# A four-layer image network on one core: the gate products of layer 3 leave layer 1's turns for the stages around layer 0

## The chip, the core and the metric

The kernel is one launch on 1 core of one Trainium2 chip. The metric is device time in microseconds of a whole launch; a time given for a kernel is the median of several runs. Engines are named as in the profile: PE (TensorE, products), PEld (its weight loads), DVE (VectorE), ACT (ScalarE), POOL (GpSimd) and SP (SyncE, which here issues most DMAs).

## What is computed

The input is x of shape (4, 64, 64, 128) in float32: four images of 64 x 64 pixels with 128 channels. Four layers follow each other on each image.

- Layer 0: attention of each pixel to its 7 x 7 neighbours (4 heads of 32), times a sigmoid gate, plus the input.
- Layer 1: group norm, then full self-attention over the 4096 pixels, plus the input.
- Layer 2: a gated product with sums over image rows, an output product, and a layer norm.
- Layer 3: a block with a depthwise 3 x 3 convolution and a selective scan in four directions. The change concerns its second half of columns, z, and where it is made:

```python
def _L3_conv_ref(x, Win, conv_w, conv_b, Wxproj, ...):      # D_INNER = 256
    xz = x @ Win                                   # (4, 64, 64, 512)
    xb, z = jnp.split(xz, 2, axis=-1)
    xb = conv3x3_depthwise(xb, conv_w)             # 256 channels
    xb = jax.nn.silu(xb + conv_b)                  # "u" in the kernel
    ...                                            # x_dbl, four scans over the pixels: y
    y = (y0 + y1 + y2 + y3)
    zf = jax.nn.silu(z.reshape(Bb, L, Cd))         # the gate
    yz = y * zf
    ...                                            # layer norm over the 256 channels
    out = yn @ Wout
```

The gate z of a pixel needs only the output of layer 2 at that pixel, and it is not used before the scans are done.

## The kernel before

**Tiles.** An image is 4096 pixels by 128 channels, in 8 chunks of CH = 512 pixels, or NT = 32 tiles of 128. Layer 0 takes 32 blocks of 8 x 16 pixels in a pipelined loop, `for i in range(-3, NT + 5)`, in which scores, softmax, value products and the projection of neighbouring blocks overlap; it is a Python generator, of which the first 8 steps (`take_in` of two chunks) can be drawn ahead of the rest. Its last iterations make the statistics and the input hT of layer 1. Layer 1 starts with one chain: mean and variance of groups (`pm` L582, `pvar` L590), Sqrt (`sd` L593), `ga` L595, then normalised hT (L605) and the products for q, k and v (L607 to L614). Then 16 query blocks follow, each of 16 groups of score products (`sc` L638), a softmax whose exponentials stand in `st` (L665), and value products (`po` L674). The scores of one block and the values of the block before overlap.

**Turns.** Layer 1 calls `between(i)` after each 8 groups, with i from 0 to 33; the main loop calls it for the turns after layer 1 (34 to 37, between pairs of `take_in` steps of the next image; for the last image 34 to 42). A turn holds other layers' work that lies beside layer 1's products: one of the four parts of layer 2 for one chunk (`turn`, `mix`, `add`, `norm`: transposes, gates, an output product, Sqrt, then the chunk x3 stored to memory, L783), and one part of layer 3's front. Layer 2 starts at turn 6, so chunk n of image b is complete from turn 4n + 9 on, and the last ones after layer 1.

**Layer 3's front.** `front(b)` returns `turn(i)`. In image b's layer 1 it works at chunks 4 to 7 of image b-1 and 0 to 3 of image b, four turns for each: `load` fetches x3 of the chunk from memory into xc (L816), `project` makes the first half of the products (`pi` L822) and copies them to xh, `convolve` runs the convolution: nine taps of a chunk on ACT (`begin` L865, `multiply` L880 and L884), on POOL (L892) and on DVE (`add_taps` L901). In the chunk's fourth turn, `gate` makes the two products `pz` (L851), applies Silu (`zf` L843) and stores zf (L855), and the next chunk's xc is loaded. Seven turns after its start, `activate` makes u by Silu (L843), `lower` the product for x_dbl (`pd` L963, `dq` L968, stores at L970), a broadcast row `bb` loaded back or made by PE, du (L983, stored into y by SP, or added into it by POOL), and `times_b` makes u times B and stores it (L994). Layer 3's second half runs after all images and reads these from memory.

The last image's chunks 4 to 7 are handled by `end(i)`, which makes their gates from x3k, still on the chip; the change leaves these four as they are. `takes` says which chunks' projections belong to which four turns; image b's front takes (b-1,4) and (b-1,5) in turn 0. `front(b)` and `turn(-1)`, which loads xc for these two, come after layer 0 of image b is issued.

**Order.** The program is a list of instructions for each engine, made from the order of the Python calls by a scheduler which may move instructions of one engine past each other; those marked `keep_in_program_order` keep their order among each other. Layer 0's instructions carry this mark (`pin`), and so do the Silu activations of `gate` and `activate` (L842 to L845), so that u and zf keep the order of the source. An engine works through its list in order; one waiting instruction holds those behind it. An activation function from another table than the one before costs an ACT_TABLE_LOAD; Silu, Sqrt and Exp each bring their own here.

**Buffers.** The pool `tmp` hands out buffers by tag in turn. Tag "c512" has 9 buffers of 128 x 512 float32 (256 KB) for prT (layer 0), x2T, sg, o and x3 (layer 2), and gsum, zf, du, u1 and bb (layer 3). A tile that gets a buffer waits for what last read it, be it an engine or a store. The products share three rings in PSUM; `pz`, `pi`, `pq`, `pk`, `pg`, `pl`, `py` and `sc` use the one with 4 buffers.

Of the kernel before, what the change touches and what calls it, by code (L numbers as in the profile page):

```python
# [22 lines left out]
F32 = mybir.dt.float32  # L23
# [6 lines left out]
P = 128  # L30
B, H, W, C = 4, 64, 64, 128
L = H * W
NT = L // P
BR, BC = 8, 16
CH = 512
# [103 lines left out]
def layers_0_to_2(  # L139
    ctx, tc, xf, mata, matb, rows, rpb, convw, sel, ident, cl, dram, big, ring, early, x3_d, ub_d, zf_d, y_d, dbl_d, ct_d, gw_d, bw_d  # L140
):
    nc = tc.nc
    wp = ctx.enter_context(tc.tile_pool(name="wa", bufs=1))
    tmp = ctx.enter_context(tc.tile_pool(name="tmp", bufs=2))
# [216 lines left out]
    def layer_0(b, xt, edge_t):  # L361
# [7 lines left out]
        gate = sml.tile([P, NT], F32, name="gate", tag="gate", bufs=2)  # L369
# [4 lines left out]
        def pin(ins):  # L374
            return tc.keep_in_program_order(ins)
# [61 lines left out]
        def statistics(n):  # L437
            pin(nc.vector.bn_stats(st[:, n, :], hT[:, bass.ts(n, CH)]))
# [106 lines left out]
        for i in range(-3, NT + 5):  # L545
            if i + 3 < NT:
                score(i + 3)
            if b == 0 and i < 1:
                load_x(0, xt, (4 * i + 28, 4 * i + 32), kept=True)
            if 0 <= i - 1 < NT:  # L550
                value(i - 1)
            if 0 <= i + 1 < NT:
                normalise(i + 1)
            if 0 <= i - 2 < NT:
                project(i - 2)
            if 0 <= i < NT:
                by_key(i, 0, nc.scalar.copy)
                by_key(i, 1, nc.vector.tensor_copy)
            if 0 <= i + 2 < NT:
                soften(i + 2, (0, 1))  # L560
            n, part = divmod(i + 3, 4)
            if n + 2 < NCH or (n + 2, part) == (NCH, 0):
                take_in(n + 2, part)
            if 0 <= i < NT:
                by_key(i, 2, nc.scalar.copy)
            if 0 <= i + 2 < NT:
                soften(i + 2, (2, 3))

            n, part = divmod(i - 6, 4)
            if 0 <= n < NCH and part == 0:  # L570
                hand_on(n)
            if 0 <= n < NCH and part == (1 if n < NCH - 1 else 0):
                statistics(n)
        handed[b] = hT, st


# [216 lines left out]
    def by_image_rows(t):  # L793
        return t.rearrange("p (i j) -> p i j", j=W)

    def front(b):
# [1 line left out]
        xh = wp.tile([P, 2, 2, RC + 2, W], F32, name="xh", tag="be")  # L798
        accs = [wp.tile([P, 2, CH], F32, name=f"acc{k}", tag=f"bm{2 * k}") for k in range(2)]
        u0 = wp.tile([P, 2, CH], F32, name="u0", tag="bm1")  # L800
        x_of, parts_of, sums, u_of = {}, [], {}, {}

        def at_end(i, n):
            return i == B - 1 and n >= 4
# [6 lines left out]
        def load(i, n):  # L811
            if at_end(i, n):
                x_of[i, n] = fresh.pop(n)
                return
            x = x_of[i, n] = tmp.tile([P, CH], F32, name="xc", tag="g1")
            nc.sync.dma_start(x, x3_d[i][:, bass.ts(n, CH)])  # L816

        def project(i, n):
            me = n & 1
            for f in range(2):  # L820
                pi = ps_s([P, CH], "pi")
                nc.tensor.matmul(pi, lhsT=win[:, P * f:P * f + P], rhs=x_of[i, n], start=True, stop=True)  # L822
                nc.scalar.copy(xh[:, me, f, 1:RC + 1, :], by_image_rows(pi))
            row = nc.vector if at_end(i, n) and n > 5 else nc.gpsimd
            if n == 4 and i < b:
                nc.gpsimd.tensor_copy(xh[:, me, :, 0, :], kept_row)
            elif n > 0:
                row.tensor_copy(xh[:, me, :, 0, :], xh[:, 1 - me, :, RC, :])
                row.tensor_copy(xh[:, 1 - me, :, RC + 1, :], xh[:, me, :, 1, :])
# [15 lines left out]
                tc.keep_in_program_order(ins)  # L845

        def gate(i, n):
            x = x_of.pop((i, n))
            for f in range(2):
                pz = ps_s([P, CH], "pz")  # L850
                nc.tensor.matmul(pz, lhsT=win[:, DI + P * f:DI + P * f + P], rhs=x, start=True, stop=True)  # L851
                zf = tmp.tile([P, CH], F32, name="zf", tag="c512", bufs=9)

                silu(i, n, zf, pz)
                nc.sync.dma_start(zf_d[i][f][:, bass.ts(n, CH)], zf)  # L855

        def tap(n, f, dy, dx):
            r0, r1, c0, c1 = region(n, dy, dx)
# [137 lines left out]
        def turn_c(i, part):  # L996

            if part == 0:
                ct = x_of["c"] = tmp.tile([W, 2, W], F32, name="ct", tag="gb")
                nc.sync.dma_start(ct[:, 0, :], by_image_rows(dbl_d[i][RANK + 1:RANK + 2, :])[0])  # L1000
            else:
                ct = x_of.pop("c")
                pt = ps_t([W, W], "pt3")
                nc.tensor.transpose(pt, ct[:, 0, :], ident[0:W, 0:W])
                nc.scalar.copy(ct[:, 1, :], pt)
                nc.sync.dma_start(by_image_rows(ct_d[i])[0], ct[:, 1, :])
# [25 lines left out]
        takes = [[(b - 1, 4), (b - 1, 5)], [(b - 1, 6)], [(b - 1, 7)]] if b > 0 else [[], [], []]  # L1032
# [12 lines left out]
        def end(i):  # L1045
# [6 lines left out]
            if i == 31:  # L1052
                gate(c, 5)
# [39 lines left out]
        def turn(i):  # L1093

            j, r = divmod(i, 4)
            add_parts()
            if i == -1:
                for c in takes[0]:
                    load(*c)
                return  # L1100
            now = whole[j] if j < 8 else None
            if j < 8:
                if r == 0:
                    for c in takes[j]:
                        project(*c)
                    if j == 7 and b < B - 1:
                        project_row(b, 4)
                if now and j < 7:
                    convolve(*now, (r // 2,), r & 1)
                elif now and r < 2:  # L1110
                    convolve(*now, range(2), r)
                if r == 3:
                    for c in takes[j]:
                        gate(*c)
                    for c in takes[j + 1] if j < 7 else []:
                        load(*c)

            for k, at in ((0, 16), (2, 28), (4, 32)):
                if i == at and whole[k] and whole[k][0] & 1:
                    copy_du(*whole[k])  # L1120
            if b > 0 and i == 8 and (b - 1) & 1:
                copy_du(b - 1, 2)

            for c, at in zip(whole, u_at):
                if c and i == at:
                    activate(*c, at >= 32)
                if c and i == at + 1:
                    lower(*c)
                if c and i == at + 2 and not by_product(*c):
                    times_b(*c, x_of.pop((*c, "b")), nc.gpsimd)  # L1130
            if b > 0 and i in (22, 24):
                turn_c(b - 1, (i - 22) // 2)
            if b == 0 and i == 3:
                output_weights()
            if b == B - 1 and i == 6:
                diagonals()
            if b == B - 1:
                end(i)

        return turn  # L1140

    coming = layer_0(0, x_next, edge_of[0])
    for _ in range(8):
# [2 lines left out]
    ahead = [x_next]  # L1146
    for b in range(B):
        xt = ahead.pop(0)
        for _ in coming:
            pass  # L1150
        if b == 0:
            for t, d in zip(bias_m, bias_d):
                nc.sync.dma_start(d, t)
        parts = layer_2(b, xt)

        def between(i):

            n, part = divmod(i - 6, 4)
            if i == 6 and b + 1 < B:
                ahead.append(load_x(b + 1))  # L1160
            if i >= 6 and n < NCH:
                parts[part](n)
            first_part(i)
            if b + 1 < B and i == NT + 1:
                edge_of[b + 1] = edge_bias(0)
            if b + 1 < B and i == NT + 3:
                bias_m[:] = bias_tiles()
                for t, d in zip(bias_m, bias_d):
                    nc.sync.dma_start(t, d)

        first_part = front(b)
        first_part(-1)
        layer_1(b, xt, *handed.pop(b), between)
        if b + 1 < B:
            coming = layer_0(b + 1, ahead[0], edge_of[b + 1])
        for i in range(NT + 2, NT + 6 if b + 1 < B else NT + 11):
            between(i)
            if b + 1 < B:
                next(coming)
                next(coming)  # L1180
# [380 lines left out]
```

## Time and profile before

| | before |
|---|---|
| median of 3 runs | 3655.63 us (3653.8 to 3657.22) |
| the profiled execution | 3657.49 us, of which the span of instructions is 3655.7 us |
| granted PE clock, mean | 0.915 |
| PE, ACT, DVE busy | 3293.8, 2619.3, 2773.2 us |
| layer 1 of images 0 to 3, first score to last value product | 525.3, 541.4, 540.9, 546.3 us |
| from there to the next image's first layer 0 score | 22.2, 24.0, 23.1 us |
| after image 3's layer 1, to the first product of the scan stage | 62.8 us (2957.2 to 3020.0) |
| last softmax of layer 0 to layer 1's first score, images 1 to 3 | 36.2, 35.0, 34.9 us |

The page gives for each engine its busy time and its share of the span, then the span in 40 equal slices of 91.4 us with the busy share in tenths. The four blocks of layer 1 fill most of the first 33 slices, and the scans the last seven. Durations used below are those of single instructions in this one execution. In the lists by line and in the timelines, an arrow with an engine and a line after an idle time names what released the waiting instruction. A product of 512 columns stands as two records of about 0.59 us that overlap.

### The profile page before, as it was taken

Reading aid. Unit: us, or ns where it says so; the run is one execution under the profiler, and the core shown is the slowest. Engines: PE = TensorE matmul, PEld = TensorE weight load, DVE = VectorE, ACT = ScalarE, POOL = GpSimd, SP = SyncE. Lnnn points to the kernel's source line nnn. Section 1 sums busy time; section 2 is a strip of 40 time slices with the busy share of each in tenths; the row PEclk is TensorE's granted clock in tenths of the full one; section 3 lists DMA queues with packets and bytes.
Section 4 is the critical chain, followed back from the end, with each engine's and each line's share of the span. In section 5 each row is a group of like instructions: output and inputs, shape, how many; then the busy total and the mean of one; then the engine's idle time right before and its main releaser. Section 6 shows DMA issues by size and latency. Waiting matters only on the chain. (4 is left out here: it accounts for less than half of the span.)

```text
span 3655.7 us, 61448 instructions
## 1 busy us (share of the span) xinstructions
PE 3293.8 (90%) x22234; PEld 2603.0 (71%) x22234; DVE 2773.2 (76%) x5070; ACT 2619.3 (72%) x4324; POOL 1416.7 (39%) x1592
## 2 busy tenths in 40 slices
PE   7999999999999999998999999989999987666647
PEld 4679988866788888666888886668888852222246
DVE  5757777767768777677787776767877768999968
ACT  4855667778667777686676777866767759999934
POOL 6500012245112222451122224521222338999856
PEclk8999999999999999999999999999999995555579
DMA  4200000131001012410021213100100279999998
GB/s 123 73 25 3 12 18 27 54 100 35 24 27 45 27 45 87 135 39 24 24 79 30 77 54 101 40 1 24 45 30 34 69 225 211 214 238 217 201 275 284
DMA packets 189362, 310.38 MB, mean 85 GB/s; under 512 B 23007, under 2 KB 111996, under 8 KB 184156
## 3 DMA queue, kind: packets, MB, share of 16 engines
q1 hardware_dynamic: 146260, 220.27, 18.0%
q0 software_dynamic: 24384, 76.95, 11.9%
q10 hardware_dynamic: 18416, 9.24, 0.9%
q8 instruction: 176, 2.88, 0.3%
q14 instruction: 126, 1.03, 0.1%
HBM read 167.69 MB, written 155.56 MB: 88 GB/s over the span
## 5 line engine op out<-in xcount | busy, mean ns | idle before, releaser
L674 PEld LDWEIGHTS po<-v,st 128*128 128x128 f32 x8192 | 1049.2, 193 | 73.5 <-issue 35.7
L674 PE MATMUL po<-v,st 128*128 128x129 f32 x8192 | 1067.8, 277 | 17.6 <-ACT st L665 17.6
L638 PE MATMUL sc<-qT,kT 128*128 128x256 f32 x4096 | 1025.7, 382 | 12.7 <-DVE mx L644 12.5
L642 ACT COPY st<-sc 128x512 f32<-128x512 f32 x1024 | 580.5, 587 | 454.2 <-PE sc L638 452.6
L644 DVE TENSOR_TENSOR mx<-mx,sc 128x512 f32<-128x512 f32 x896 | 613.2, 684 | 275.7 <-ACT st L642 252.3
L638 PEld LDWEIGHTS sc<-qT,kT 128*128 128x128 f32 x4096 | 718.9, 191 | 105.7 <-issue 13.9
L664 DVE TENSOR_TENSOR st<-st,pb 128x2048 f32<-128x2048 f32 x256 | 572.4, 2280 | 29.0 <-PE pb L661 28.7
L665 ACT ACTIVATE st<-st 128x2048 f32<-128x2048 f32 x256 | 484.6, 1910 | 28.5 <-DVE st L664 27.2
L1271 PE MATMUL pdt<-dbl,dt 8*128 8x512 f32 x512 | 307.5, 1081 | 142.3 <-ACT de L1278 141.7
L1282 POOL TENSOR_TENSOR inp<-de,ub 128x1024 f32<-128x1024 f32 x128 | 409.6, 4391 | 6.8 <-ACT de L1278 6.3
L1271 PEld LDWEIGHTS pdt<-dbl,dt 8*128 8x128 f32 x512 | 114.2, 312 | 332.8 <-ACT de L1278 270.0
L505 POOL TENSOR_SCALAR pr<-pr,sm 128x308 f32<-128x308 f32 (+3 forms) x512 | 243.9, 496 | 205.1 <-DVE sm L503 186.8
L746 POOL TENSOR_TENSOR x<-x,row 128x512 f32<-128x512 f32 x32 | 47.9, 1498 | 707.1 <-DVE mx L644 686.7
L892 POOL TENSOR_TENSOR gsum<-gsum,tp 128x504 f32<-128x504 f32 (+1 forms) x177 | 229.2, 1301 | 127.1 <-ACT gsum L880 73.8
L497 ACT ACTIVATE pr<-pr,mx 128x308 f32<-128x308 f32 (+3 forms) x512 | 262.8, 517 | 1.3 <-DVE mx L486 1.3
L1309 DVE TENSOR_TENSOR_SCAN h<-h,end,inp 128x1024 f32<-128x1024 f32 x96 | 221.1, 2346 | 20.3 <-ACT h L1295 9.7
L514 PE MATMUL pt<-ident,pr 128*88 128x128 f32 (+5 forms) x1472 | 205.4, 276 | 9.8 <-ACT prT L516 8.8
L901 DVE SCALAR_TENSOR_TENSOR acc<-xh,cc,acc 128x512 f32<-128x512 f32 (+3 forms) x250 | 199.5, 803 | 10.2 <-ACT acc L865 8.6
L1324 POOL DMA_DIRECT2D y<-yo x112 | 200.6, 2710 | 13.1 <-DMA y<-y 4.8
L742 POOL TENSOR_TENSOR o<-o,rt 128x512 f32<-128x512 f32 x32 | 34.3, 1070 | 438.9 <-DVE o L741 434.4
L514 PEld LDWEIGHTS pt<-ident,pr 128*88 128x88 f32 (+5 forms) x1472 | 164.6, 138 | 45.2 <-ACT prT L516 25.9
L483 DVE CUSTOM_DVE_ANT_0 pr<-sc,bias_m 128x266 f32<-128x266 f32 (+1 forms) x384 | 152.1, 452 | 56.7 <-PE sc L479 55.1
(235 smaller groups left out, 4964.8 us busy)
## 6 DMA issues: line engine op xcount, KB each, us to landing
y<-yo POOLq DMA_DIRECT2D x112, 512.0 KB, 10.4
y<-y SPq DMA_DIRECT2D x48, 512.0 KB
zf_d<-zf SPq DMA_DIRECT2D x64, 256.0 KB
ub_d<-u SPq DMA_DIRECT2D x64, 256.0 KB
ub<-ub_d SPq DMA_DIRECT2D x16, 1024.0 KB
yl<-y SPq DMA_DIRECT2D x64, 256.0 KB
zc<-zf_d SPq DMA_DIRECT2D x64, 256.0 KB
v_d<-vg SPq DMA_DIRECT2D x128, 64.0 KB
```

Source lines behind the costliest of these rows:

```text
L497: pin(nc.scalar.activation(k.pr[:, h], k.pr[:, h], AF.Exp, bias=k.mx[:, h:h + 1], accum_out=k.sm[:, h:h + 1]))
L505: nc.gpsimd.tensor_scalar(k.pr[:, h], k.pr[:, h], k.sm[:, h:h + 1], 1.0, ALU.mult, ALU.mult)
L514: pin(nc.tensor.transpose(pt[0:n, h, :], k.pr[:, h, at:at + n], ident))
L638: nc.tensor.matmul(ps[:, r, :], lhsT=kT[:, bass.ts(G * g + r, P)], rhs=qT[:, bass.ts(i, QB)], start=True, stop=True)
L642: nc.scalar.copy(st, ps)
L644: nc.vector.tensor_tensor(k.mx, group(ng * i) if g == 1 else k.mx, ps, ALU.max)
L664: nc.vector.tensor_tensor(part, part, pb.unsqueeze(1).to_broadcast([P, 4 * G, QB]), ALU.add)
L665: nc.scalar.activation(part, part, AF.Exp)
L674: nc.tensor.matmul(k.po[:, h, :], lhsT=st[:, r, bass.ts(h, P)], rhs=v[:, j, :], start=(j == 0 and h == 0), stop=(j == NT - 1 and h == 1))
L892: nc.gpsimd.tensor_tensor(a, a, p, ALU.add)
L1271: nc.tensor.matmul(pdt[j][:, g, :], lhsT=dt[o:o + RANK, P * f:P * f + P], rhs=at(dbl[o:o + RANK, :], k & 2, g0, g0 + CH), start=True, stop ...
L1282: nc.gpsimd.tensor_tensor(by_rows(inp), by_rows(de), at(ub_s[f], b ^ (k & 1), SC * n, SC * n + SC), ALU.mult)
```

## The change

- 28 of the 32 chunks' gates move: all but those of the last image's chunks 4 to 7.
- Gates of (b, 0 to 3) go to turns 34 to 37 (NT + 2 to NT + 5), that is after image b's layer 1. Gates of (b-1, 4 to 7) go to iterations NT - 1 to NT + 2 of image b's layer 0, near its end.
- Since xc is given up after its projection, a new function `fetch` loads x3 of the chunk once more into a tile xg, tag "c512": 28 more DMAs of 256 KB on SP, at turns 32 and 33 (two each) and at iterations NT - 3 (two), NT - 1 and NT (one each).
- The projection of (b-1, 4) goes from turn 0 to iteration NT + 2 of layer 0. `front(b)` for b > 0 is made at iteration NT - 4, and xc for its first two chunks is loaded at NT - 3.
- To make this possible, `layer_0` yields i at the end of each iteration below NT + 4.

```diff
@@ layer_0
                 statistics(n)
+            if i < NT + 4:
+                yield i
@@ front: project
+            if not at_end(i, n):
+                x_of.pop((i, n))
@@ front: gate
-            x = x_of.pop((i, n))
+            x = x_of.pop((i, n)) if at_end(i, n) else fetched.pop((i, n))
@@ front: new
+        def fetch(i, n):
+            x = fetched[i, n] = tmp.tile([P, CH], F32, name="xg", tag="c512", bufs=9)
+            nc.sync.dma_start(x, x3_d[i][:, bass.ts(n, CH)])
@@ front: turn
-            if i == -1:
-                for c in takes[0]:
-                    load(*c)
-                return
...
                     for c in takes[j]:
-                        project(*c)
+                        if c != (b - 1, 4):
+                            project(*c)
...
                 if r == 3:
-                    for c in takes[j]:
-                        gate(*c)
+                    if j == 7 and b == B - 1:
+                        gate(b, 4)
...
+            if i in (NT, NT + 1):
+                for n in range(2):
+                    fetch(b, 2 * (i - NT) + n)
+            if NT + 2 <= i < NT + 6:
+                gate(b, i - NT - 2)
...
-        return turn
+        def ahead_of(i):
+
+            if i == NT - 3:
+                for c in takes[0]:
+                    load(*c)
+                fetch(b - 1, 4)
+                fetch(b - 1, 5)
+            if i in (NT - 1, NT):
+                fetch(b - 1, i - NT + 7)
+            if NT - 1 <= i < NT + 3:
+                gate(b - 1, i - NT + 5)
+            if i == NT + 2:
+                project(b - 1, 4)
+
+        return turn, ahead_of
@@ main loop
-        for _ in coming:
-            pass
+        for i in coming:
+            if b > 0 and i == NT - 4:
+                first_part, ahead_of = front(b)
+            if b > 0 and i is not None and i > NT - 4:
+                ahead_of(i)
...
-        first_part = front(b)
-        first_part(-1)
+        if b == 0:
+            first_part, _ = front(b)
         layer_1(b, xt, *handed.pop(b), between)
```

In the order of the built programs, PE, DVE and POOL have as many instructions after as before, ACT has 260 table loads instead of 237, and SP 1322 DMAs instead of 1294.

More of the change, by code (lines that the diff above doesn't have):

```diff
@@ L800, in front @@
         u0 = wp.tile([P, 2, CH], F32, name="u0", tag="bm1")
-        x_of, parts_of, sums, u_of = {}, [], {}, {}
+        x_of, parts_of, sums, u_of, fetched = {}, [], {}, {}, {}
         def at_end(i, n):
```

## The prediction

> **What bounds the kernel now.** I read the engines' totals and the slices first, then a table of windows by stage, then the timelines of the stages that the change touches. The page's first lines:
>
> ```profile
> PE 3293.8 (90%) x22234; PEld 2603.0 (71%) x22234; DVE 2773.2 (76%) x5070; ACT 2619.3 (72%) x4324; POOL 1416.7 (39%) x1592
> ...
> PEclk8999999999999999999999999999999995555579
> ```
>
> PE is the fullest engine, and its clock is granted nearly whole until the scan at the end. An average hides that stages differ, so I cut the span at events: layer 1 from its first score to its last value product; the "tail" from there to the next image's first layer 0 score; the "drain" from layer 0's last softmax to layer 1's first score. The columns of the table: window, its length, busy time of PE, PEld, DVE, ACT, POOL, then granted clock, DMA share, GB/s.
>
> ```profile
> 941.60:1483.00 541.40, 527.32 (x3472) 467.58 (x3471) 417.12 (x603) 389.44 (x519) 126.62 (x112) 0.99 0.15 45
> 747.10:769.30 22.20, 17.20 (x92) 11.02 (x91) 12.16 (x34) 9.72 (x15) 5.40 (x10) 0.92 0.51 163
> 1483.00:1507.00 24.00, 19.08 (x98) 12.44 (x97) 13.06 (x39) 10.39 (x17) 7.03 (x12) 0.86 0.85 239
> 2957.20:3020.00 62.80, 52.34 (x237) 26.68 (x234) 30.83 (x54) 28.08 (x47) 24.05 (x22) 0.89 0.89 248
> 905.40:941.60 36.20, 31.51 (x173) 20.25 (x172) 14.11 (x31) 15.93 (x26) 1.84 (x5) 0.86 0.00 1
> ```
>
> Layer 1 of image 1 (first row) keeps PE busy 527.32 of 541.40 us, 97.4%, with ACT at 72%: there, a product taken out is time taken out. Image 0's layer 1, with 4 gates and 4 projections fewer, says the same: its row has 512.50 of 525.30, 15 us less PE work and 16 us less time. Drains and tails are chains between engines with PE idle 5 us in each; image 3's tail moves data 89% of its time.
>
> **What is taken out of layer 1.** All 28 gates that read xc leave it: 4 in image 0, 8 in each other image (32 records in image 1: two per product, two products per gate).
>
> ```profile
> L851 PE MATMUL pz<-xc,win 128*128 128x512 f32 x32 | 15.0, 592 | 0.0
> L843 ACT ACTIVATE zf<-pz 128x512 f32<-128x512 f32 x16 | 8.6, 595 | 0.1
> ```
>
> A product of 512 columns takes 0.86 us of PE: in the tail's timeline below, pl, pk and pv start at 753.33, 754.19 and 755.05. A gate is 1.72. The projection of chunk (b-1,4), two such products, leaves layer 1 too in three images: (28+3) x 1.72 = **-53.3 us** (by the row's busy time, 15.0/8 = 1.88 a gate, -58.3). Before the first value product of image 1, PE stands 4.83 us behind DVE, whose queue held seven convolution taps of 0.74; three of them move to the drain. That is 3 x 0.74 = 2.2 in three images, 6.6 if all of it ended late; image 0's stall, without those taps, is 3.14. I take half, -3.3 (0 to -9.6). Layer 1 together: **-56.6**, from -53 to -68.
>
> It does not get simpler for ACT. In the changed order u's Silu is no longer pinned behind a gate, and stands 15 to 20 score groups earlier, no longer beside layer 2's Sqrt: the table loads rise from 237 to 260 rather than fall, at 1283 ns. About 8 of the net increase lie in layer 1, 10 us, against 28 x 2 x 0.6 = 33 us of zf that leave. ACT waited 105 us for scores there, so I price this at 0; uncovered it is up to 10.
>
> **What comes back in the drains (images 1 to 3).** Four gates and a projection, 5 x 1.72 = 8.6 us of PE, stand before layer 1's statistics. The timeline of image 1 (start, duration, what; in brackets idle before and its releaser):
>
> ```profile
> 912.34 0.33 PE L434 MATMUL pt<-ident,x 128*128 128x128 f32 x1
> 912.70 0.59 ACT L435 COPY hT<-pt 128x512 f32<-128x512 f32 x1 [1.35 <-PE pt L434]
> ...
> 914.48 0.59 PE L582 MATMUL pm<-mv,ma 128*128 128x1 f32 x2 [1.81 <-DVE mv L579]
> ...
> 916.58 0.20 ACT L593 ACTIVATE sd<-sd 128x1 f32<-128x1 f32 x1 [1.99 <-DVE sd L592]
> 916.81 0.16 DVE L595 RECIPROCAL ga<-sd 128x1 f32<-128x1 f32 x1 [0.27 <-ACT sd L593]
> ...
> 917.81 2.08 PE L607 MATMUL pq<-hT,ma 128*128 128x512 f32 x2 [1.46 <-DVE hT L605]
> ```
>
> It is one chain, hT, mv, pm, pvar, sd, ga, hT, pq; nothing runs beside it. The new products fill the 1.81 before pm and some 0.7 earlier, so pm comes 6.1 later. ACT gets, behind hT, two zf, two xh copies, a begin of 0.82, a tap of 0.71 and the Sqrt load, 5.0 in all: sd comes at about 924.0, +7.4. DVE has the three taps ahead of ga: **+8.2** a drain, 24.6 in three; ends 6 (PE alone) and 9.5 (all products plus 0.9). The fetches cost nothing: SP's queue and the DMAs are idle there (0.00), and the fetches stand one block or two, some 4 us each, ahead of their products.
>
> **What comes back in the tails (images 0 to 2).** 4 x 1.72 = 6.9 us of PE, 8 zf, and two more Silu loads on ACT's way. Image 0, before:
>
> ```profile
> 749.57 0.43 SPq L783 DMA_DIRECT2D x_d<-x  x1
> 750.64 0.59 ACT L391 COPY xT<-pt 128x512 f32<-128x512 f32 x1
> 751.62 0.82 SPq L987 DMA_DIRECT2D y<-du  x2
> 753.33 1.02 PE L738 MATMUL pl<-x2T,w_le 128*128 128x512 f32 x2
> 754.19 1.02 PE L402 MATMUL pk<-xT,ma 128*128 128x512 f32 x2
> 754.44 0.69 ACT L740 ACTIVATE o<-pl,b_le 128x512 f32<-128x512 f32 x1 [0.22 <-DMA dbl_d<-dq]
> 754.53 0.96 SPq L994 DMA_DIRECT2D ub_d<-u  x2
> 755.05 1.46 PE L413 MATMUL pv<-ma,xT 128*128 128x192 f32 x8
> 760.48 0.30 ACT L762 ACTIVATE rd<-mv,eps 128x4 f32<-128x4 f32 x1 [3.25 <-DVE mv L760]
> 760.80 1.28 ACT L426 ACT_TABLE_LOAD   x1
> ```
>
> The cost is less the products than the buffers. prT0, x2T, sg, o, x3, zf, du, u and bb share nine buffers, and now the fetched xg too. In the changed order x2T and the first product wait for the first fetch, the first zf for the x3 store (749.57), the second for the landing of the first y<-du, o for the first ub_d store, the fourth zf for the store of the first. On SP the first two fetches stand ahead of the second load of bias_m and the x3 store; that load waits until 749.21 for a ub_d store anyway, so I price this at 0. The next image's xT, qT, kT and layer 2's o stand behind them on ACT, and PE's pq, pg and py wait for those. y<-du is issued at 751.62; a bb of this size took 3.7 us to be seen by its user (740.41 to 744.12), an accumulating y<-du 5.7. So the second zf goes at 755.3 to 757.3, and xT at about 756.2 instead of 750.64: **+5.6**. The ub_d store, issued at 754.53, has landed by then, so o keeps +5.6, and so do py and rd. Behind rd a Silu load and two zf (1.28 + 1.1) stand before the second xT: +8.0. A second Silu load and two zf stand between its qT and kT; PE's own pz and cold pv (1.86) covered some of that: the first score comes **+8.4**. In image 1 the accumulating y<-du and the other images' copies hold the queues (DMA 0.85): I add 3, **+11.4**. Three tails: 28.2. Ends: 5 each, 15 (PE's 6.9 less some of its idle, no late landing), and 14 to 17 each, 46 (landings 6 us later still).
>
> At image 3's tail, PE gets 6.9 more in a stretch that ends at the scan's first product; a zf must wait for POOL's accumulating y<-du, which already ended ACT's wait for u at 2971.10. **+8**, from 4 (the 10 us of idle take some) to 14.
>
> **Two rules.** The table load at 760.80 is followed by its activation at 762.09: a switch costs the load alone, 1.28. The Trainium skill (ScalarE: Activation LUTs, What ACT_TABLE_LOAD costs) puts it at about 2.66 us, with a drain of 1.38 beside the load; the trace shows no such drain. By the page, two loads in each of three tails and one in each drain would add 9 x 1.38 = 12 us, an estimate. In image 0's tail pq, pk and pv took 1.62, 1.91 and 1.86 after an idle of 2.88, against 1.12, 1.02 and 1.46 before it. The skill's page TensorE: Matmul & The Clock Gate (What's actually happening) halves the clock after an idle window of about 3.4 us; the trace shows the loss after less. Filling that hole would, by the rule, bring back 1.8 us a tail, 5 in all, an estimate. I take neither.
>
> **Sum.** -56.6 + 24.6 + 28.2 + 8 = **+4.2 us** on the profiled execution (3657.49; span 3655.7 and 1.8 around it): 3661.7. The median of the runs lies 1.9 lower, so 3660.
>
> **Rivals.** *Faster*: the landings come before their users, and xT waits for nothing. Then tails cost 5, drains 6 and the last tail 5: -56.6 + 18 + 15 + 5 = -18.6, about 3637. For it: DMA is only half busy in tails 0 and 2. Against it: y<-du is issued after xT used to start, whatever its landing takes. It decides if the first y<-du lands before about 752.
> *Slower*: the ub_d store lands late. Its place is o in each tail, since o, py, rd and the second xT follow it in a row; price 1 us per us, three times. From 760 on (it is issued at 754.5) it takes the lead from xT; at 766 they add 6 a tail, 18: +22, about 3678. For it: in image 1 DMA is nearly full, four fetches and eight stores add 3 MB to each tail, where image 0's had 163 GB/s for 22 us, 3.6 MB, and SP issues in order. Against it: 0.5 MB in 9 us is slow for queues at half load.
> *It doesn't do what it says*: the freed ACT and PE time in layer 1 is lost to the added table loads (10 us): 3670.
>
> **How the numbers follow.** A measurement tells 0.2%, 7.3 us: from 3648 to 3663 is no change. The forecast, 3651 to 3669, 0.45; faster 0.22; late stores 0.20; loads uncovered 0.13. The forecast's lower two thirds are within 0.2%, the rest slower: faster 0.23, same 0.30, slower 0.47. The range, 3640 to 3679, leaves out some of the faster case and the far end of the slower.
>
> **What would show it.** Layer 1 of images 1 to 3 should be 16 to 17 us shorter (525, 524, 530), image 0's 7; drains 44 instead of 36; tails 30 to 35; the last one 71. In the tails, xT of the next image waits behind a zf whose releaser is a DMA, y<-du. If layer 1 shrinks by less than 14, the table loads or a new stall took it, and the first part is wrong; if a zf waits only for PE, the tails are.

## The result and the profile after

The changed kernel takes **3749.68 us** (median of 5 runs, 3742.38 to 3753.21) where the one before takes 3655.63 (median of 5 too): ratio 1.025, with a 95% interval of 1.0238 to 1.0261. The forecast was 3660 with a range of 3640 to 3679, so it was wrong: the change costs 2.5%. The profiled execution took 3749.76 us, of which the span is 3748.0 (before 3657.49 and 3655.7), so the span grew by 92.3. The page of after, engines' totals and granted clock:

```profile
PE 3313.8 (88%) x22234; PEld 2616.7 (70%) x22234; DVE 2835.9 (76%) x5070; ACT 2656.3 (71%) x4347; POOL 1426.6 (38%) x1592
...
PEclk8999999999999999999999999999999995555579
```

With the same 22234 products PE is busy 20 us longer, and DVE 63 us longer with the same 5070 instructions: some of them became slower. The windows of after that answer to those shown of before (layer 1 of image 1, tails of images 0, 1 and 3, drain of image 1; same columns):

```profile
959.50:1503.60 544.10, 515.99 (x3436) 464.05 (x3436) 430.95 (x596) 384.25 (x502) 129.72 (x111) 0.99 0.12 37
743.40:779.60 36.20, 26.67 (x101) 14.63 (x99) 11.03 (x31) 17.45 (x26) 5.42 (x10) 0.81 0.56 183
1503.60:1540.80 37.20, 26.46 (x98) 14.51 (x96) 10.98 (x31) 17.41 (x26) 6.67 (x12) 0.82 0.83 265
3033.70:3112.00 78.30, 59.78 (x253) 30.43 (x251) 31.31 (x54) 32.41 (x55) 24.03 (x22) 0.89 0.85 249
917.00:959.50 42.50, 37.96 (x193) 23.09 (x192) 19.63 (x39) 24.89 (x41) 2.32 (x6) 0.92 0.19 69
```

Layer 1 of image 1 lost the products and PE's busy time there fell by 11.3 us, yet the stage became 2.7 us *longer*: PE stood idle 28.1 us instead of 14.1. The tails of images 0 to 2 lasted 1.6 to 1.7 times as long, those of images 0 and 1 at a clock of 0.81 and 0.82 instead of 0.92 and 0.86. All stages, cut at the same events in both traces (here a tail ends where the next image's first score, or the scan's first product, starts; before's rows ahead of this section, and after's row for image 3, run 1.5 to 2.5 us past that):

| us | before | after | change | predicted |
|---|---|---|---|---|
| layer 1, images 0, 1, 2, 3 | 525.2, 541.3, 540.9, 546.2 | 521.2, 543.9, 545.1, 551.4 | **+8.0** | -56.6 |
| drains, images 1 to 3 | 36.4, 35.0, 34.9 | 42.6, 42.6, 41.9 | **+20.8** | +24.6 |
| tails, images 0 to 2 | 20.7, 21.6, 20.7 | 36.1, 37.3, 33.0 | **+43.4** | +28.2 |
| tail of image 3 | 60.7 | 76.4 | **+15.7** | +8 |
| layer 0 of image 3 | 137.4 | 141.4 | **+4.0** | 0 |

They add up to 91.9 of the 92.3. Nearly three quarters of the error is layer 1. The next lines show what PE waited for there, and what DVE, which it waited for, was busy with. They are groups of layer 1 of image 1, before and then after (idle time and its releaser behind the last bar):

```profile
L901 DVE SCALAR_TENSOR_TENSOR acc<-xh,cc,acc 128x504 f32<-128x504 f32 (+2 forms) x64 | 50.7, 794 | 1.1 <-ACT acc L865 0.6
L661 PE MATMUL pb<-dm,ones 128*128 128x256 f32 x32 | 10.5, 409 | 6.0 <-DVE dm L657 5.3 <-DVE rd L763 0.4
L647 DVE TENSOR_TENSOR mx<-mx 128x256 f32<-128x256 f32 x16 | 6.8, 422 | 0.3
```

```profile
L909 DVE SCALAR_TENSOR_TENSOR acc<-xh,cc,acc 128x504 f32<-128x504 f32 (+3 forms) x56 | 51.2, 924 | 0.9 <-ACT acc L873 0.6
L663 PE MATMUL pb<-dm,ones 128*128 128x256 f32 x32 | 10.7, 416 | 18.3 <-DVE dm L659 17.6 <-ACT st L644 0.6
L649 DVE TENSOR_TENSOR mx<-mx 128x256 f32<-128x256 f32 x16 | 11.3, 705 | 0.4
```

`pb` broadcasts a block's row maxima and stands in PE's list; `dm` comes from DVE at the end of each of 16 blocks, behind the fold `mx<-mx` (which joins the two halves of the running maxima) and the maximum `nm`. PE now waits 18.3 us before `pb` instead of 6.0. The fold itself takes 705 ns instead of 422, a tap 924 instead of 794. The end of the same block in before's timeline and then in after's (start, duration, what; in brackets idle before):

```profile
1323.68 0.42 DVE L647 TENSOR_TENSOR mx<-mx 128x256 f32<-128x256 f32 x1
1323.71 1.53 POOL L746 TENSOR_TENSOR x<-x,row 128x512 f32<-128x512 f32 x1 [20.56 <-DVE mx L644]
1326.51 0.42 DVE L654 TENSOR_REDUCE nm<-pt 128x2 f32<-128x256 f32 x1 [1.54 <-PE pt L652]
1328.22 0.67 PE L661 MATMUL pb<-dm,ones 128*128 128x256 f32 x2
```

```profile
1340.46 1.81 DVE L909 SCALAR_TENSOR_TENSOR acc<-xh,cc,acc 128x504 f32<-128x504 f32 x1
1341.70 4.74 POOL L900 TENSOR_TENSOR gsum<-gsum,tp 128x504 f32<-128x504 f32 x3
1342.20 1.47 DVE L649 TENSOR_TENSOR mx<-mx 128x256 f32<-128x256 f32 x1
1344.19 2.79 DVE L909 SCALAR_TENSOR_TENSOR acc<-xh,cc,acc 128x504 f32<-128x504 f32 x2
1346.90 0.41 DVE L656 TENSOR_REDUCE nm<-pt 128x2 f32<-128x256 f32 x1
1347.83 0.55 DVE L659 TENSOR_SCALAR dm<-ident,nm 128x128 f32<-128x128 f32 x2
1348.53 0.67 PE L663 MATMUL pb<-dm,ones 128*128 128x256 f32 x2 [2.39 <-DVE dm L659]
```

In after, taps stand ahead of the fold and, two of them, between fold and maximum. POOL adds `gsum` beside them: the tap ahead of the fold takes 1.81 us instead of 0.73, the fold 1.47 instead of 0.42, the two taps behind it 2.79, while `nm` and `dm` take as long as ever. At these ends, every second one, before's list has nothing between fold and maximum but a sum of layer 2. At the others before has one tap and layer 2's statistics there, and after the statistics and four normalisations.

### The profile page after: what moved, and what is told of

The parts are those of the page before. It is cut to its first block, busy times and chain, and to the rows that moved or that the text cites. A ratio compares the mean times of both kernels' runs of the same rounds, so it can differ in the third digit from the quotient of the medians.

```text
span 3748.0 us, 61449 instructions
## 1 busy us (share of the span) xinstructions
PE 3313.8 (88%) x22234; PEld 2616.7 (70%) x22234; DVE 2835.9 (76%) x5070; ACT 2656.3 (71%) x4347; POOL 1426.6 (38%) x1592
## 5 line engine op out<-in xcount | busy, mean ns | idle before, releaser
L1309 POOL TENSOR_TENSOR inp<-de,ub 128x1024 f32<-128x1024 f32 x128 | 413.8, 4498 | 12.8 <-DMA ub_d<-u 8.7
L909 DVE SCALAR_TENSOR_TENSOR acc<-xh,cc,acc 128x512 f32<-128x512 f32 (+3 forms) x250 | 219.0, 886 | 4.7 <-ACT acc L873 3.1
```

The source lines that it names most:

```text
L1309: nc.gpsimd.tensor_tensor(by_rows(inp), by_rows(de), at(ub_s[f], b ^ (k & 1), SC * n, SC * n + SC), ALU.mult)
```

## The experiments

Ratios are to the kernel before, run beside each experiment; in brackets stands the 95% interval. Stage times come from one profiled execution of each kernel.

**Theory: DVE's list in layer 1** ("order" in the expectations). The pinned Silu of a gate held its chunk's work in place; without it the scheduler puts the convolution's work some 16 groups earlier, where its taps fall on the block ends. In image 1 the projections stand at the same score groups in both traces (48, 80, 112 and on), while `begin` of the chunks behind them moves from groups 76, 108 and 140 to 56, 93 and 124. Rival ("cover"): the products moved out only lay on top of waits that PE has anyway, so their loss gains nothing. First, DVE's list was pinned to the source's order, in after (e1) and in before (e2):

```diff
+                tc.keep_in_program_order(
                     nc.vector.tensor_tensor(k.mx, ...)        # score maxima
+                tc.keep_in_program_order(
                     nc.vector.tensor_scalar(x, x, mv[:, k, 0:1], rd[:, k:k + 1], ...)   # norm
+                tc.keep_in_program_order(
                     nc.vector.scalar_tensor_tensor(acc, x, c, acc, ALU.mult, ALU.add)   # taps
```

> The changed kernel, with three kinds of DVE instructions of layer 1's stretch kept in program order (the running maxima mx, the convolution taps, layer 2's normalisation): none of these taps and normalisations then stands in DVE's list between a block's last maximum (the fold) and dm. Theory 'order': layer 1 gained nothing because in the changed list taps and normalisations stand there, so PE waits for pb at the ends of blocks (18 us in image 1's layer 1 instead of 6) and its clock drops after it. Then layer 1 of images 1 to 3 falls from 544, 545 and 551 us to 524 to 530, and the total from 3750 to 3690 to 3700. Theory 'cover': the wait for dm was always there and the gate's products, taken out, only lay on top of it. Then layer 1 stays at 540 to 550 and the total within 10 us of 3750.

> The kernel before with the same three kinds of DVE instructions kept in program order, as the control of the run above. Theory 'order': before has few such instructions at its block ends and 14 us of idle PE in a layer 1, of which at most 8 are at the ends of blocks and in the first block: 2 to 8 us less in each layer 1, total 3625 to 3648. Theory 'cover': nothing changes, 3655 within 7.

e1: 3755.0, 1.0256 (1.024 to 1.0271). e2: 3704.65, 1.0118 (1.0103 to 1.0133). Neither went as the theory expected: e1 is where the rival had it, and e2 is slower than both allowed. As a cure this is inconclusive, since the pins alone cost before 45 us. With nearly equal DVE lists, though, layer 1 with the gates out is shorter by 3.1, 3.4, 3.0 and 7.0: less than the 7 and 16 to 17 predicted, but shorter. e12 pins only the norm in after:

> The changed kernel with only layer 2's four normalisations of a chunk kept in program order on DVE; the running maxima and the taps stay free. In the list the normalisations then stand behind dm at every second end of a block, and the taps stay where the changed kernel has them. Theory 'order', with the normalisations priced apart: the five waits of 1.09 us at these ends go, 5 to 6 us in each layer 1 of images 1 to 3, total 3730 to 3737; the rest of the loss is the taps and their sharing with POOL. If the normalisations are not the cause of these waits, the total stays within 5 us of 3750.

3743.05, 1.0235 (1.022 to 1.0251), 6 to 13 above what was expected. In its profiled execution, the fastest of its four (3733.35, the others 3743 to 3745), layer 1 is 6.1, 5.0, 6.6 and 2.9 shorter than after's. The waits for pb that were to vanish shrank only from 1.09 to 0.91 each, since statistics of `add` (layer 2) still stand ahead.

**One half of the change at a time.** e4 keeps the gates of chunks 0 to 3 in their turns and moves only what goes to the drains; e11 keeps those of 4 to 7 and the projection, and moves only what goes to the tails. Fetches go with the gates.

```diff
 e4, turn: r == 3
-                    if j == 7 and b == B - 1:
-                        gate(b, 4)
+                    for c in takes[j]:
+                        if c[0] == b:
+                            gate(*c)
 e11, turn: r == 3
+                    for c in takes[j]:
+                        if c[1] > 3:
+                            gate(*c)
```

> Half of the change: only the gates of (b-1, 4 to 7) and the projection of (b-1, 4) move, to the drains; the gates of (b, 0 to 3) stay in layer 1's turns and nothing is added to the tails. The drains should cost 6 to 7.5 us each as in the changed kernel, 21, and the tails be those of before. In layer 1, four gates and a projection (8.6 us) leave the first half only. Theories 'order' and 'cover' both expect the ends of blocks to go late in that half alone; by the changed kernel's halves the gain is about eaten up: layer 1 of images 1 to 3 at 541 to 544, total 3673 to 3685. If the drains' half keeps its gain, layer 1 is at 533 and the total at 3650 to 3655.

> The other half of the change: only the gates of (b, 0 to 3) move, to the tails; those of (b-1, 4 to 7) and the projection stay in the turns. It closes the account. Theory 'order': DVE's list goes late in the second half of each layer 1, from which these gates came, by more than the 6.9 us that they took: from the changed kernel less the drains' half, layer 1 of images 1 to 3 at 547 to 551 (555 in image 3), longer than before although it has less work; tails as in the changed kernel, +12 to +16 each, the last one +14 to +16; total 3728 to 3748. Theory 'cover': taking work out can't lengthen layer 1, which stays at 541 or below, total at or below 3715.

e4: 3666.65, 1.0023 (1.0013 to 1.0032), between the two outcomes expected; layer 1 of images 1 to 3 is 4.4 to 5.4 shorter, the drains cost 6.6 to 8.2 each. e11: 3735.2, 1.0216 (1.0202 to 1.023); layer 1 of images 1 to 3 is 550.4, 548.9, 552.0, and that of image 0 is 4.3 shorter than before's. Windows of layer 1 of image 1 and its pb row, first e4, then e11:

```profile
947.40:1483.20 535.80, 520.03 (x3451) 465.26 (x3450) 412.65 (x595) 382.92 (x505) 126.89 (x111) 0.99 0.14 42
```

```profile
L663 PE MATMUL pb<-dm,ones 128*128 128x256 f32 x32 | 10.6, 412 | 9.0 <-DVE dm L659 8.5 <-DVE rd L765 0.4
```

```profile
951.00:1501.50 550.50, 524.11 (x3455) 467.02 (x3454) 434.21 (x604) 391.01 (x515) 127.77 (x110) 0.99 0.13 41
```

```profile
L663 PE MATMUL pb<-dm,ones 128*128 128x256 f32 x32 | 10.6, 414 | 15.3 <-DVE dm L659 15.2
```

In e4, PE's busy time falls by 7.3 and the stage by 5.4: there a product out is nearly its time out. In e11 it falls by 3.2, and the stage grows by 9.1: cover that is lost can't lengthen a stage, so the rival alone can't explain it. The waits before pb add up: e4 has 3.0 more than before, e11 9.3, after 12.3. So the tails' half of the change does most of the harm to layer 1.

**Placeholders.** e5 leaves at each gate's old place two products and two pinned Silu of 8 columns, whose result nothing uses; e6 does so in e4:

```diff
+        def hold(i, n):
+            x = x_of.pop((i, n))
+            for f in range(2):
+                pz = ps_s([P, 8], "ph")
+                nc.tensor.matmul(pz, lhsT=win[...], rhs=x[:, 0:8], start=True, stop=True)
+                silu(i, n, sml.tile([P, 8], F32, name="hz", tag="hz"), pz)
...
                     for c in takes[j]:
+                        (gate if at_end(*c) else hold)(*c)
```

> The changed kernel, in which each moved gate leaves a placeholder at its old place in layer 1's turns: the same two products and two Silu, in the same pinned order, but on 8 columns instead of 512, with the result unused. DVE's list then has no normalisation between fold and dm, as in the kernel before, and only the taps that before had there. Theory 'order': what cost layer 1 its gain is the new list, not the missing work. Then layer 1 of images 1 to 3 goes from 544, 545 and 551 us to 525 to 532 (before's 541 less 15.5, plus about 0.5 for each placeholder pair), and the total from 3750 to 3695 to 3710. Theory 'cover': the gates' work lay on waits of PE that were there anyway, so a list as before's doesn't bring the gain back: layer 1 at 538 to 545, total at 3730 to 3755.

> Only the drains' half of the change (gates of (b-1, 4 to 7) and that chunk's projection), with the same placeholders for these gates in the turns. Without placeholders this half gave layer 1 of images 1 to 3 at 535.9, 535.9 and 541.8 and a total of 3667, 7 above the kernel before. Theory 'order': the ends of blocks that went late in its first half come back to before's, layer 1 at 530 to 533 (536 to 538 in image 3), total 3650 to 3658. Theory 'cover': no gain, 534 to 538 and 3660 to 3670.

e5: 3708.32, 1.0138 (1.0117 to 1.0158), 41 us below after. e6: 3664.4, 1.0021 (1.0012 to 1.003), as e4 within its interval, which is what the rival expected: its wait before pb is back at 6.1, but PE waits 1.9 longer for the score maxima than in e4 and is busy 1.6 longer. Layer 1 of image 1 in e5:

```profile
954.80:1488.90 534.10, 518.05 (x3467) 465.96 (x3467) 413.55 (x595) 380.32 (x514) 126.51 (x111) 0.99 0.13 38
```

```profile
L663 PE MATMUL pb<-dm,ones 128*128 128x256 f32 x32 | 10.5, 409 | 7.2 <-DVE dm L659 6.6 <-DVE rd L765 0.5
L649 DVE TENSOR_TENSOR mx<-mx 128x256 f32<-128x256 f32 x16 | 6.8, 424 | 0.3
```

With more work on PE and ACT, layer 1 is 4.3, 9.9, 13.9 and 9.7 shorter than after's. The wait is back at 7.2 and the fold at 424 ns; `begin` stands at groups 76, 108 and 141 again, and DVE's list at the block ends is nearly before's. This shows that the place of the convolution's and layer 2's work, not the amount of PE's, took 38 us. Against before, layer 1 of the four images is then 30 us shorter, about half of the 56.6 forecast: with the list put back, and the placeholders in it, the products were still not worth their full time.

**The turns moved.** Calls four groups *earlier* (the names and expectations of these three runs say later, which is wrong), in after (e7), before (e9) and e4's kernel (e10):

```diff
-            if (s % 8 == 7 or s == ng * (NB + 1) + LAG - 1) and t > 0:
+            if s % 8 == 3 and t > 0:
```

> The changed kernel with layer 1's turns called 4 groups later in each half block (after group 3 instead of 7 of eight). Taps and normalisations then stand in DVE's list beside the scores of a block, and almost none between fold and dm. No work is added or taken out. Theory 'order': layer 1 of images 1 to 3 falls to 525 to 536, total 3690 to 3715 (the tails may change by a few us, since the last turns start earlier). Theory 'cover': the waits for dm stay as they are, layer 1 at 540 to 550.

> The kernel before with layer 1's turns called 4 groups later in each half block, as in the changed kernel that gained 70 us from it. Here the list is good already: about 8 of the 14 us of PE's idle in a layer 1 are at the ends of blocks and in the first block. Theory 'order': 0 to 8 us less in each layer 1, total 3625 to 3657, and where new waits come, they are for the fold or nm with a normalisation or tap ahead of them. If the phase of the turns helps for another reason (the last turns' place before the tails), the tails get shorter too, below 20 us.

> Only the drains' half of the change, with the turns 4 groups later. Without the shift it took 3667, 7 above before: layer 1 gave back 5 each, the drains took 7 to 8 each. Theory 'order': its layer 1 still has 8.7 us of waits for dm in image 1 and 4 in the first block; without them 528 to 534, total 3640 to 3660. 'Cover': 534 to 540, total 3660 to 3675.

e7: 3679.17, 1.0061 (1.0046 to 1.0076). e9: 3777.95, 1.033 (1.0316 to 1.0344). e10: 3744.35, 1.0237 (1.0223 to 1.0251). The same shift takes 70 us from one list and adds 121 to the other, where a small gain was expected. Of the 70, layer 1 gives 38 and the four tails 36, so e7 is not a test of layer 1 alone. In e9 PE waits for the score maxima instead of pb; layer 1 of image 1:

```profile
L638 PE MATMUL sc<-qT,kT 128*128 128x256 f32 x1024 | 260.7, 390 | 23.1 <-DVE mx L644 22.5
L901 DVE SCALAR_TENSOR_TENSOR acc<-xh,cc,acc 128x504 f32<-128x504 f32 (+2 forms) x64 | 69.8, 1094 | 1.6 <-ACT acc L865 1.1
```

Here a tap costs 1094 ns, so by place alone 64 taps cost 19 us more. e13 and e14 move only the last turns in before (30 to 33 of image 3; 32 and 33 of all), to look for a gain in the tail:

> The kernel before, in which only the last image's turns 30 to 33 are called after group 3 of their eight instead of group 7 (that is 4 groups earlier; the two runs named turns_later moved all turns in this direction too). With all turns moved, image 3's tail took 52 us instead of 61 while layer 1 got 36 to 46 us longer in images 1 to 3. Theory 'order': the tail's gain comes from the last turns alone, as they start before layer 1's products end, and layer 1 keeps before's list: tail 52 to 57, layer 1 of image 3 at 546 to 550, total 3646 to 3655. If the gain needs the whole shift, 3653 to 3660.

> The kernel before, in which the turns 32 and 33 of every image are called after group 3 of their eight instead of group 7. With all turns moved, the tails of images 0 to 2 took 19.6 to 20.3 us instead of 20.7 to 21.6, and the last one 52 instead of 61. If the last two turns make this gain, tails 19.5 to 20.5 and the last one 53 to 58, total 3644 to 3654; if not, 3653 to 3660.

3657.57, 0.9997 (0.9989 to 1.0006) and 3663.41, 1.0023 (1.0014 to 1.0031): in e13 image 3's tail falls to 52.6 and its layer 1 rises to 553.7. No gain.

**DVE beside POOL.** e15 (after) and e16 (before) let POOL's adds work on 8 of 504 columns, in the same order; they leave those sums of the convolution out.

```diff
-                nc.gpsimd.tensor_tensor(a, a, p, ALU.add)
+                nc.gpsimd.tensor_tensor(a[:, 0:1, 0:8], a[:, 0:1, 0:8], p[:, 0:1, 0:8], ALU.add)
```

> The changed kernel, in which POOL's additions of the convolution's parts (gsum<-gsum,tp, 1.3 us each) cover 8 columns of one row instead of the chunk, with the same order and waits on every engine; the rest of these sums is left out, so the convolution's output is not the reference's. DVE's list, with taps and normalisations ahead of nm and dm, is that of the changed kernel. Theory 'port': in the changed list taps, fold and normalisations fall on POOL's additions, and those of DVE's instructions that read two tiles in SBUF, or scale one, wait for POOL's to end (taps of 0.73 us take 1.43, folds of 0.42 take 1.06 while POOL is busy). Then the waits for dm of 2.4 us at every second end go, and layer 1 of images 1 to 3 falls by 8 to 14 us, to 530 to 536 (538 to 543 in image 3). Theory 'list alone': the entries ahead of nm are as many, so layer 1 falls by less than 4.

> The kernel before with the same reduced additions on POOL, as the control: the same work is left out. Its taps fall on POOL's additions less often (4 of 64 wholly, against 15 of 56). Theory 'port': layer 1 falls by 0 to 4 us only, so the changed kernel gains more from this than before does by 6 to 10 in each layer 1. Theory 'list alone': both fall by the same.

e15: 3687.11, 1.0082 (1.0065 to 1.0098); e16: 3617.88, 0.9898 (0.9883 to 0.9912). Layer 1 of the four images falls by 60 us in after and by 37 in before, where only 0 to 4 an image were expected (it is 7 to 12). The difference, 23 us of what the change lost, goes with POOL's additions. That they hold DVE's instructions up is seen at the fold below; what comes from POOL itself being done earlier was not separated from it. With POOL's adds small in both, the change does shorten layer 1, by 3.1 to 4.8 an image, 15 in all instead of 57. e15, image 1:

```profile
L663 PE MATMUL pb<-dm,ones 128*128 128x256 f32 x32 | 10.5, 410 | 7.9 <-DVE dm L659 7.8
L649 DVE TENSOR_TENSOR mx<-mx 128x256 f32<-128x256 f32 x16 | 6.8, 423 | 0.4
```

The fold is at 423 ns again, and the wait at 7.9, with the list unchanged.

**The tails.** e3 gives their zf two buffers of their own; e8 also stores no zf there (it stores x3 in its place, earlier, and leaves those gates out of the output):

```diff
+                if n < 4 and b < B - 1:
+                    zf = tmp.tile([P, CH], F32, name="zf", tag="g1")
+                else:
+                    zf = tmp.tile([P, CH], F32, name="zf", tag="c512", bufs=9)
```

> The changed kernel, in which the gates in the tails of images 0 to 2 put zf into the two buffers of xc, which are free then, instead of the shared nine. The first two zf then wait for no store. Theory 'landing': the tails' price is the wait of zf for the landing of an x3 or y store, with xT and PE's pq behind it, and the slow clock after PE's idle 5.3 us. Then xT goes 3 to 4 us after x2T's transposes instead of 7, pq at the full clock, and each of the three tails is 6 to 8 us shorter: total 3726 to 3734. Theory 'work': the price is the products, the eight zf and the table loads themselves. Then the tails stay within 3 us each and the total at 3741 to 3750.

> The changed kernel without any DMA behind the zf of images 0 to 2's tails: these zf go into xc's two buffers and are not stored; the gates of chunks 0 to 3 of these images are left out of the output (x3 is stored in their place, in layer 1). The eight products and eight zf stay in each tail. Theory 'landing': the tails' price is zf waiting for DMAs (3.3 us for the first, 5.9 in the run with own buffers) and the slow clock after PE's idle. Then the tails go from 36, 37 and 33 us to 27 to 31, total 3730 to 3737. Theory 'work': 33 to 36 each, total at 3742 to 3752.

e3: 3748.79, 1.024 (1.0224 to 1.0255), tails 35.7, 36.7, 35.8: nothing gained. e8: 3734.22, 1.0211 (1.0195 to 1.0226), tails 29.3, 32.6, 29.3. Tail 0 in after's timeline, then e3's:

```profile
752.20 1.25 ACT L847 ACTIVATE zf<-pz 128x512 f32<-128x512 f32 x2 [3.31 <-DMA x_d<-x]
753.35 0.58 ACT L391 COPY xT<-pt 128x512 f32<-128x512 f32 x1
753.98 2.08 PE L395 MATMUL pq<-xT,ma 128*128 128x512 f32 x2 [5.28 <-ACT xT L391]
756.14 2.05 PE L736 MATMUL pg<-x2T,ma 128*128 128x512 f32 x2
757.99 1.91 PE L740 MATMUL pl<-x2T,w_le 128*128 128x512 f32 x2
```

```profile
749.07 1.12 PE L395 MATMUL pq<-xT,ma 128*128 128x512 f32 x2 [1.71 <-ACT xT L391]
...
758.79 1.21 ACT L847 ACTIVATE zf<-pz 128x512 f32<-128x512 f32 x2 [5.88 <-DMA zf_d<-zf]
```

In e3 xT comes early, and then the third zf waits 5.88 us for the store of the first: the wait moved. In e8, where zf waits for no transfer, the tails still cost 8.6, 11.0 and 8.6 more than before. So landings and stores are 6.8, 4.7 and 3.7 of their price. The rest is put down here to the work in ACT's and PE's chain, at the clock it then gets; no run shows that apart. Tails with buffers enough for all zf were not tried. No version that computes all of the output beat the kernel before.

## Why the prediction was wrong

**The failed step** is "there, a product taken out is time taken out", with "Layer 1 together: -56.6". It measured +8.0, which is 65 of the 90 us by which the forecast missed. The trace of before showed that PE was full, not what kept it full: a DVE list with little work at the block ends. Image 0's layer 1, with which the prediction backs this step, has 32 taps instead of 64 on DVE as well, so it could not tell products from taps. In image 1, 16.9 us of products went (15.0 in the gates' row, 1.9 for a projection), and the stage grew by 2.7. The 19.6 between are PE's idle before pb (+12.3), its other idle (+1.7), and 5.6 by which PE's busy time fell less than those rows. Some 4 of the 5.6 are a lower clock: two gaps of 4.12 and 2.38 us before pb were each followed by 3.6 us at half clock (two more of 2.39 were not); the rest may be that records overlap. e5 shows that what stands at the gates' old place sets this, e11 that the tails' half does most of it, e15 against e16 that 23 us of it go with POOL's additions. The exact split between list, slowing and clock stays open, and so does why one shift of four groups helps after and harms before, beyond the waits shown, and why e5 finds only half of the forecast gain.

That u "is no longer pinned behind a gate, and stands 15 to 20 score groups earlier" stood in the prediction and was priced on ACT alone, by its table loads, at 0. It was the right observation on the wrong engine: DVE's taps moved with it.

**Drains**: +6.2, +7.6, +7.0 against +8.2 each, a little less than forecast and for the reason given: PE is busy 37.96 of 42.50, one chain with the products in it. In image 1 pm comes 5.2 later (forecast 6.1) and sd 6.3 later (forecast 7.4).

**Tails 0 to 2**: the kind of wait was right, the transfer named was not, and the size was too small by 15. Tail 0, counted from the last value product:

| | before | after | change | predicted |
|---|---|---|---|---|
| first xT | 3.6 | 9.9 | +6.4 | +5.6 |
| o | 7.4 | 16.5 | +9.1 | +5.6 |
| rd | 13.4 | 23.8 | +10.4 | +5.6 |
| second xT | 15.2 | 28.0 | +12.8 | +8.0 |
| first score | 20.7 | 36.1 | +15.4 | +8.4 |

xT waits behind a zf that a DMA released, as forecast, but the DMA is the x3 store, x_d<-x (3.31, 2.84 and 2.30 in the three tails). The y<-du that the prediction named held a zf for 0.35 alone, in tail 2, and in tail 1 it held x2T for 3.23. So it is in part luck that the first row comes within 1 us. The first miss is between xT and o: PE had been idle 5.28, and pq, pg and pl then took 2.08, 2.05 and 1.91 where before they took 1.12, 1.10 and 1.02: 2.8 us. The Trainium skill (TensorE: Matmul & The Clock Gate, What's actually happening) halves the clock after an idle window of about 3.4 us; the prediction cited it as speaking for the change, in an idle that it would fill, but the late xT made a longer one. In e3, after an idle of 1.71, pq took 1.12. Another 1.3 lies between o and rd, where a gate's products (2.17) now stand ahead of py in PE's list. The last miss, 2.2, is in the last step: pq at half clock again (2.08, after 2.79 idle, less than the page's window), and the Silu load and two zf ahead of kT were not covered.

**Tail 3**: +15.7 against +8, outside its 4 to 14. The waits of after (total, times, longest):

```profile
ACT zf L847 <- DMA y<-du: 9.8, 1, 9.8
PE pb L983 <- ACT dq L976: 8.8, 4, 7.1
ACT x2T L298 <- DMA y<-du: 7.2, 1, 7.2
```

A landing, POOL's accumulating y<-du, was forecast to hold one zf within the slack; it held x2T as well, twice in ACT's list, 17 us.

**Layer 0 of image 3**, not predicted: a stretch of it at a lower clock, below.

**Rivals.** *Slower* named one place, o behind the ub_d store, 3678: in tail 0 o was released by PE (pl), not by that store, so this mechanism did not decide. *Doesn't do what it says* came nearest: layer 1's gain was lost, but to DVE's order, not to table loads. *Faster* failed with the landings. The range was too narrow, because the gain in layer 1 was in every case and no case had its list rearranged.

## What to carry to other kernels

Work taken from the fullest engine can be lost again when the other engines' lists change with it: compare the changed lists around each wait of that engine, on all engines, before counting a product as time. Pins are part of a schedule; when a pinned instruction moves, price whatever it held in place. In the tails here a wait for a landing cost its own length (3.31), the clock after it (2.8), and, once the first was taken away, the next wait on a ring of buffers (5.88).

## What the runs showed of the hardware

**DVE beside POOL.** In layer 1 of image 1, five of after's 16 folds begin while a `gsum` addition of POOL runs. Each ends 0.28 us after that addition and takes 0.85 to 1.47 us instead of 0.42. In before, seven folds have an addition `x<-x,row` of POOL that begins 0.03 us behind them, and they take 0.42. So a fold was held by an addition that had begun, not by one that began second (one fold of 0.42 in after has an `x<-x,row` whose record begins 0.67 ahead of it; why it isn't held is open). Those of after's instructions that lie beside POOL for four fifths of their time or more take on average: taps 1.43 us instead of 0.73, the norm 1.32 instead of 0.34, dm 0.90 instead of 0.28. The maxima from PSUM (0.68) and `st+=pb` (2.28) don't change. 15 of 56 taps lie so in after, 4 of 64 in before. The Trainium skill (SBUF — State Buffer, SBUF: two separate sides) tells of a port pair that DVE and GpSimd share as an exclusive lock, for DVE operations with two SBUF inputs or in a two-port mode; the rows agree, but for that one fold.

**Clock without a gap.** In layer 0 of image 3, a window of after:

```profile
2302.00:2312.00 10.00, 9.79 (x32) 4.84 (x31) 5.09 (x31) 5.94 (x20) 5.82 (x15) 0.55 0.22 63
```

PE is busy 9.79 of 10 us at a granted clock of 0.55, with no idle over 0.21 us in the 9 us before it. Some 4 us went this way, in 12 of the 27 layer 0's that follow a tail with gates (after, e1, e5, e7, e11, e12 and e15 have them, e3 and e8 none), and in none of the 27 that follow a tail without. Why is open.
